# A nested Strassen step for the last setup product, and the rows of mp stored batch by batch in the loop: gated cross-attention with RMSNorm in fp32

## The chip, the cores and the metric

One core of a Trainium2 chip. The metric is the device time of one execution in microseconds (us), lower is better. All data and all arithmetic are fp32.

## The reference, cut to what matters

```python
# x: (8, 1024, 1024)   ctx: (8, 64, 512)   W_mem: (1024, 512)   W_gate: (1024, 2048)
mp     = einsum('bme,de->bmd', ctx, W_mem)                      # 8 x 64 rows of 1024
scores = einsum('bnd,bmd->bnm', x, mp) / sqrt(1024)
attn   = softmax(scores)
mctx   = einsum('bnm,bmd->bnd', attn, mp)
gate   = sigmoid(einsum('bnf,df->bnd', concat([x, mctx]), W_gate) + b_gate)
fused  = x + gate * mctx
out    = fused * rsqrt(mean(fused**2) + 1e-6) * norm_w          # norm_w is all ones
```

The half of the gate product that takes `mctx` is folded: `mg = mp @ W2` (W2 is the lower half of the transposed W_gate) is computed once for all 512 rows of memory, so that in the loop `attn @ mg` stands for `mctx @ W2`. What remains large is `x @ W1`, 8192 x 1024 x 1024.

## The kernel before, in words

**Setup** (to about 81 us). The memory is transposed on the TensorE. `mp` is then computed in transposed form, in four tiles `mpT[r][h]` (also called `m11`, `m12`, `m21`, `m22`), by one Strassen step of seven products (`pm_product`). `mg` is computed by a second one-level Strassen step, again seven products (`mg_product`, eight matmuls of 128x512 each), in the order 1, 6, 5, 2, 7, 4, 3, into the four tiles `c11`, `c12`, `c21`, `c22`. Its operands `t1`, `t2`, `b12` are sums of quarters of W2, which POOL makes (`w2_sum`), and `b21 - t2`, which DVE makes in place, in four pieces, ahead of product 4. The last product, number 3, is `s2` times `b22`, and is added to `c12`.

Beside that run the preparations of the loop. W1 is split into seven Strassen operands, of which four are outer sums: `outer_sum(5..)`, `(7..)`, `(6..)`, `(4..)`, one DVE instruction of 128x2048 each. Each operand `o` gets four inner sums for a second Strassen level, written to a tile `it{o}` (`inner_sum`, 128x512 each): for `o` = 1, 7, 5, 6, 4 on POOL in the setup, for 2 and 3 on DVE in the first pass of the loop. x comes in `xq` tiles of 512 rows (four transfers of 512 KB by `load_xq`); DVE transposes them in 32x32 blocks by STREAM_TRANSPOSE (`transpose_x`), eight instructions a tile, into `A` tiles that take the places of the `mpT` tiles in the setup. `outer_s` (DVE, 128x1024) and `inner_s` (POOL, 128x256) make the left sums.

**mp's two layouts in DRAM.** `store_mpT` writes the `mpT` tiles to the scratch `mpd`, from which `load_mp(b)` reads one batch for the scores. `store_mp(g)` transposes 128 rows (two batches) by two STREAM_TRANSPOSE on DVE and writes them by four DMAs of 128 KB into the scratch `mgd`; before, all four groups are done in the setup, between products 1 and 6. `store_mg` adds mg to `mgd`, and `load_mg(b)` brings both of a batch to the tile `mgs[b]`: rows of mp on partitions 0 to 63, rows of mg on 64 to 127.

**Loop.** Sixteen passes `q`, called quads, of 512 rows of x, two for each batch. A quad is seven outer products in the order 1, 6, 7, 5, 4, 2, 3; each is `outer_product`, an inner Strassen step of seven products A, B, C, D, A again, E, F, two matmuls of 128x256 each, and each such product is a *slot*; a quad has 49. Work of other engines is put by hand at slots (`at(t0 + 49, ...)` is the first slot of the next quad) or beside a product (`mid`). The five PSUM banks b0 to b4 take A to F in rotation, with F in the bank of B: so F can't start before DVE has made `u2` from B. In the first product of the first quad A, B, C, D, E take b0, b1, b2, b3, b4.

The setup's products take eight banks in turn (`setup_bank`): b0 to b4, two of the pool for contexts, and the one for scores. A product of the setup that uses b0 to b4 must therefore be read out before a quad's product of the same bank starts.

**Order.** All engines run what they are given in program order (`pin`). `mm` (line 92) is every matmul, `tt` (line 95) every tensor_tensor of DVE and POOL, `load` (line 98) every DMA of the SP queue, loads and stores alike. So the profile shows these three lines for nearly everything, and tiles must be told by their names: `pg` are the banks of mg's products, `mg_c` its four results, `t<-w,t` an outer sum, `it<-..` and some `t<-t`, `w<-w` an inner sum, `w<-w,t_w` the sums `b21 - t2`, `s<-..` an `outer_s`, `l<-..` an `inner_s`.

## Time and profile before

| | |
|---|---|
| median of 3 runs | 972.62 us (972.55 to 972.7) |
| the profiled execution | 972.56 us, its span 970.8 us |
| PE busy | 959.5 us, 99% of the span |
| DVE busy | 818.4 us, 84% |
| POOL busy | 761.1 us, 78% |
| ACT busy | 328.5 us, 34% |
| DMA moved | 128.32 MB |
| granted TensorE clock | 0.996 |

The span is what the profile sees of the profiled execution; 1.76 us of its time lie around it. PE is the TensorE's matmuls, PEld its weight loads, DVE the VectorE, ACT the ScalarE, POOL the GpSimd, SP the engine that issues the DMAs. A line of the timeline gives the start in us, the length in us, the engine, the line of the kernel, the operation, output<-inputs, shapes (partitions x elements) and count; where several instructions in a row are alike they are merged.

### The profile page before, as it was taken

The numbers are of one execution on the slowest core, as the hardware profiler recorded it, in microseconds if no ns is written. First come the engines' busy times: TensorE is split into PE (matmuls) and PEld (weight loads), VectorE is DVE, ScalarE is ACT, GpSimd is POOL, SyncE is SP. The second block draws the span as 40 slices with busy tenths as digits, with TensorE's granted clock in tenths as the row PEclk, the third lists the DMA queues.
The fourth block names the chain that finished last, engine by engine and source line by source line (L and its number), as shares of the span: only waits on it lengthen the run. The fifth ranks groups of instructions, "written<-read, shape, count | busy, mean of one in ns | idle before, by whom it ended". The sixth has DMA issues, their size and how long they took to land.

```text
span 970.8 us, 14402 instructions
## 1 busy us (share of the span) xinstructions
PE 959.5 (99%) x4986; PEld 774.9 (80%) x4986; DVE 818.4 (84%) x1482; ACT 328.5 (34%) x604; POOL 761.1 (78%) x889
## 2 busy tenths in 40 slices
PE   9999999999999999999999999999999999999995
PEld 8646878788888888788888888888887878888884
DVE  6988879879797988979797978979797978979787
ACT  2000234161423334161433324152333425152345
POOL 4997878778786978878786978878687878878692
PEclk9999999999999999999999999999999999999998
DMA  9856573482919374482918375381917465391712
GB/s 378 271 141 163 98 131 98 114 169 72 178 66 166 97 144 105 108 176 66 184 65 159 102 137 113 95 188 55 195 67 146 115 129 121 87 196 48 189 69 86
DMA packets 70919, 128.32 MB, mean 132 GB/s; under 512 B 12352, under 2 KB 49216, under 8 KB 70592
## 3 DMA queue, kind: packets, MB, share of 16 engines
q1 hardware_dynamic: 61520, 93.34, 37.0%
q0 software_dynamic: 9184, 33.56, 18.9%
q8 instruction: 39, 0.64, 0.3%
q10 hardware_dynamic: 144, 0.52, 0.1%
q14 instruction: 32, 0.26, 0.1%
HBM read 87.56 MB, written 41.68 MB: 133 GB/s over the span
## 4 chain that ended last, share of the span: by engine, by line
PE 98%; DVE 1%; issue 0%; ACT 0%; DVEq 0%
PE kA L92 20%; PE pc L92 12%; PE kE L92 11%; PE kD L92 10%; PE kF L92 10%; PE kB L92 10%; PE kC L92 10%; PE psT L92 6%; PE pg L92 5%; PE pm L92 3%; PE pz L92 0%; PE pa L443 0%; PE sc L417 0%; PE pt L196 0%; DVE gate L749 0%
## 5 line engine op out<-in xcount | busy, mean ns | idle before, releaser
L95 POOL TENSOR_TENSOR gate<-gate,u 128x256 f32<-128x256 f32 x336 | 287.5, 887 | 107.5 <-DVE u L95 107.5
L662 ACT ACTIVATE gate<-gate 128x512 f32<-128x512 f32 x128 | 80.5, 631 | 306.9 <-DVE gate L95 306.1
L349 DVE STREAM_TRANSPOSE a<-xq 128x512 f32<-128x512 f32 x128 | 137.9, 1099 | 2.7 <-POOL it L95 2.7
L95 POOL TENSOR_TENSOR l<-a 128x256 f32<-128x256 f32 x128 | 122.0, 953 | 21.6 <-PE kA L92 20.4
L92 PE MATMUL pc<-mg,attnT 64*128 64x256 f32 x512 | 127.5, 389 | 0.0
L92 PE MATMUL kB<-it,l 128*128 128x256 f32 x448 | 115.1, 379 | 0.2 <-DVE gate L95 0.2
L92 PE MATMUL kD<-it,l 128*128 128x256 f32 x448 | 115.0, 379 | 0.0
L92 PEld LDWEIGHTS pc<-mg,attnT 64*128 64x128 f32 x512 | 90.6, 186 | 29.9 <-issue 21.2
L691 DVE SCALAR_TENSOR_TENSOR gate<-gate,ss,nw_sb 128x512 f32<-128x512 f32 x120 | 110.6, 931 | 1.1
L95 POOL TENSOR_TENSOR l<-s 128x256 f32<-128x256 f32 x96 | 78.0, 813 | 36.1 <-PE kF L92 35.9
L92 PE MATMUL kA<-w,a 128*128 128x256 f32 x384 | 98.6, 379 | 0.0
L92 PEld LDWEIGHTS kB<-it,l 128*128 128x128 f32 x448 | 85.0, 190 | 12.1 <-DVE gate L95 0.6
L92 PEld LDWEIGHTS kD<-it,l 128*128 128x128 f32 x448 | 85.1, 190 | 11.6
L95 DVE TENSOR_TENSOR gate<-gate,pc 128x512 f32<-128x512 f32 x128 | 86.7, 678 | 0.4 <-ACT gate L662 0.4
L95 DVE TENSOR_TENSOR gate<-gate,kE 128x256 f32<-128x256 f32 x112 | 45.5, 419 | 47.1 <-PE kE L92 41.1
L92 PEld LDWEIGHTS kA<-w,a 128*128 128x128 f32 x384 | 71.7, 190 | 9.5 <-DVE s L95 0.2
L815 ACT COPY u<-kA 128x256 f32<-128x256 f32 x112 | 40.5, 361 | 110.3 <-PE kA L92 106.0
L92 PE MATMUL kE<-it,a 128*128 128x256 f32 x256 | 69.0, 392 | 0.0
L676 ACT ACTIVATE junk<-gate 128x1024 f32<-128x1024 f32 x60 | 63.5, 1058 | 10.5 <-DMA gate<-in_x 9.5
L92 PE MATMUL kA<-t,s 128*128 128x256 f32 x256 | 65.8, 379 | 0.0
L92 PE MATMUL kC<-w,l 128*128 128x256 f32 x256 | 65.7, 379 | 0.0
L92 PE MATMUL kF<-w,l 128*128 128x256 f32 x256 | 65.7, 379 | 0.0
(140 smaller groups left out, 2041.0 us busy)
## 6 DMA issues: line engine op xcount, KB each, us to landing
xq<-in_x SPq DMA_DIRECT2D x64, 512.0 KB, 10.3
gate<-in_x POOLq DMA_DIRECT2D x60, 512.0 KB, 8.1
out<-gate SPq DMA_DIRECT2D x60, 512.0 KB, 2.6
w<-in_w_gate_t SPq DMA_DIRECT2D x8, 512.0 KB, 10.0
w<-in_w_gate_t SPq DMA_DIRECT2D x2, 2048.0 KB, 17.1
mg<-mgd SPq DMA_DIRECT2D x16, 256.0 KB, 3.8
mpd<-mpT SPq DMA_DIRECT2D x4, 512.0 KB, 7.0
mgd<-mpq SPq DMA_DIRECT2D x16, 128.0 KB, 3.6
```

The lines of the kernel that those rows point to most:

```text
L92: pin(nc.tensor.matmul(o, lhsT, rhs, start=start, stop=stop, skip_group_check=True))
L95: pin(eng.tensor_tensor(o, a, b, op))
L349: nc.vector.transpose(A[key][:, :, r * P : (r + 1) * P], chunks(xq[q][:, 4 * t : 4 * t + 4, :], KD)[:, half * KH : (half + 1) * KH],)
L662: pin(nc.scalar.activation(g, g, AF.Sigmoid))
L676: nc.scalar.activation(junk, O[q, t], AF.Square, accum_out=ss[:, t % 2 : t % 2 + 1])
L691: nc.vector.scalar_tensor_tensor(g[:, cols], g[:, cols], rstd[:, t % 2 : t % 2 + 1], nw_sb[:, cols], ALU.mult, ALU.mult,)
L815: pin(nc.scalar.copy(p1, kb["A"]))
```

## The change

Four things.

1. The last product of mg, number 3, is computed by a nested Strassen step (`mg_nested`): its 256x512 by 512x512 blocks are cut once more into quarters, and seven products of two 128x256 matmuls take the place of eight 128x512 matmuls. Its right sums `t1_` to `t4_` are eight POOL instructions of 128x256, its left sums four on DVE, both in `it2` and `it3`. Its results are gathered by one ACT copy, three DVE sums from PSUM (`u2`, `u3`, `u4`), three POOL sums into `c12`, and four DVE sums from PSUM into `c12`. `outer_s(0, 1)` stands between the DVE's `u4` and these four.
2. Only the rows of batches 0 and 1 are transposed and stored in the setup (`store_mp_pair`: two STREAM_TRANSPOSE and four DMAs in place of eight and sixteen). The rows of batches 2 to 7 are transposed from the batch's tile `mps[b]` by one STREAM_TRANSPOSE at the slot at which `load_mg` stood, into a tile `mpq` of their own, and stored by four DMAs of 64 KB (`store_mp_batch`); `load_mg` comes a slot later, so that it and the next `load_xq` follow these stores in the SP queue.
3. `load_xq(0)` is issued ahead of the stores of `mpT`, and the first four `transpose_x(0, ..)` come before the sums of product 6.
4. The order of the inner sums: on POOL, `s3` comes before `it1`; `it7` comes after the first `inner_s`; the four of `it5` move from POOL to DVE, where they stand between the outer sum 6 and the sums of product 2.

```diff
-    inner_sums(nc.gpsimd, 1)                       # after the sums of W2 on POOL
...
+    load_xq(0)
     for r, h in ((0, 0), (1, 1), (1, 0)):
         store_mpT(r, h)
...
+    def store_mp_batch(b):
+        mpq = t4k(small, [P, M // 32, Q4], "mpq", f"mpq{b}")
+        pin(nc.vector.transpose(chunks(mpq, KD), mps[b]))
+        store_mp(mpq, slice(b * M, (b + 1) * M))
...
+    def mg_nested(eng, l, r, ts, ss, o):
...
+        for k in range(2):
+            tt(eng, t1_[:, k, :], r[k][:, hi], r[k][:, lo], ALU.subtract)
+            tt(eng, t2_[:, k, :], r[2 + k][:, hi], t1_[:, k, :], ALU.subtract)
+            tt(eng, t3_[:, k, :], r[2 + k][:, hi], r[k][:, hi], ALU.subtract)
+            tt(eng, t4_[:, k, :], r[2 + k][:, lo], t2_[:, k, :], ALU.subtract)
+        tt(nc.vector, s1_, l21, l22, ALU.add)
+        tt(nc.vector, s2_, s1_, l11, ALU.subtract)
+        tt(nc.vector, s3_, l11, l21, ALU.subtract)
+        tt(nc.vector, s4_, l12, s2_, ALU.subtract)
+        yield
...
+        kb = [setup_bank(f"pn{i}")[:, :C] for i in range(6)]
...
+        product(0, l11, r11)
+        pin(nc.scalar.copy(p1_, kb[0]))
+        product(1, s2_, t2_)
+        add(u2, p1_, kb[1])
+        product(2, s3_, t3_)
+        add(u3, u2, kb[2])
+        for n in (3, 2):
+            tt(nc.gpsimd, dst[n], dst[n], u3, ALU.add)
+        product(3, s1_, t1_)
+        add(u4, u2, kb[3])
+        tt(nc.gpsimd, dst[1], dst[1], u4, ALU.add)
+        product(0, l12, r21, False)
+        product(4, l22, t4_)
+        product(5, s4_, r22)
+        yield
+        for n, b in ((0, 0), (3, 3), (2, 4), (1, 5)):
+            add(dst[n], dst[n], kb[b])
...
-    for n in range(4):
-        inner_sum(nc.gpsimd, 7, n)
+    inner_sums(nc.gpsimd, 1)
...
-    for g in (2, 3, 0, 1):
-        store_mp(g)
+    store_mp_pair()
     load_mp(0)
+    for t in range(4):
+        transpose_x(0, t, 0)
     pgs = mg_product(6, s2, t2)
     mg_sum(c21, c11, pgs)
     tt(nc.gpsimd, s2, m12, s2, ALU.subtract)
-    for t in range(4):
-        transpose_x(0, t, 0)
     for part in range(2):
         inner_s(0, 1, part)
+    for n in range(4):
+        inner_sum(nc.gpsimd, 7, n)
...
+    next(nested)
     pgs = mg_product(5, s1, t1)
     mg_sum(c12, c21, pgs)
     w1_place(6)
     outer_sum(6, 3, 5)
     for n in range(4):
-        inner_sum(nc.gpsimd, 5, n)
+        inner_sum(nc.vector, 5, n)
...
+    next(nested)
     outer_s(0, 1)
-    pgs = mg_product(3, s2, b22)
-    mg_sum(c12, c12, pgs)
+    for _ in nested:
+        pass
     store_mg(c12, 0, 1)
...
-            at(t0 + 49, load_mg, (q + 1) // QPB)
+            if q + 1 > QPB:
+                at(t0 + 49, store_mp_batch, (q + 1) // QPB)
+            at(t0 + 50, load_mg, (q + 1) // QPB)
```

## The prediction

> **What bounds the kernel now.** I read the shares and the chain that ended last first, then PE's waits, and then the timelines of PE, DVE and POOL around 60 to 87 us, where the change lies.

> ```profile
> PE 959.5 (99%) x4986; PEld 774.9 (80%) x4986; DVE 818.4 (84%) x1482; ACT 328.5 (34%) x604; POOL 761.1 (78%) x889
> ...
> PE 98%; DVE 1%; issue 0%; ACT 0%; DVEq 0%
> ```

> The TensorE is the bound from end to end. PE's waits come to two entries, 1.2 us at the start and 0.2 us once: a PE instruction taken out is gained in full, and a PE wait added is lost in full.

> ```profile
> 67.61 7.03 PE L92 MATMUL pg<-w,mpT 128*128 128x512 f32 x16
> 74.48 7.03 PE L92 MATMUL pg<-w,mp_s 128*128 128x512 f32 x16
> 81.35 1.03 PE L92 MATMUL kA<-w,a 128*128 128x256 f32 x4
> 82.21 1.03 PE L92 MATMUL kB<-it,l 128*128 128x256 f32 x4
> 83.07 1.03 PE L92 MATMUL kC<-w,l 128*128 128x256 f32 x4
> ...
> 86.53 1.03 PE L92 MATMUL kF<-w,l 128*128 128x256 f32 x4
> ```

> The first line is product 4, the second is product 3, then the first quad begins. Starts tell the pace: product 3 takes 81.35 - 74.48 = 6.87 us, a product of the loop 0.863.

> ```profile
> 57.92 2.29 DVE L95 TENSOR_TENSOR t<-w,t 128x2048 f32<-128x2048 f32 x1
> 60.12 1.51 DVE L95 TENSOR_TENSOR mg_c<-mg_c,pg 128x512 f32<-128x512 f32 x2
> 61.55 6.19 DVE L95 TENSOR_TENSOR w<-w,t_w 128x512 f32<-128x512 f32 x4
> 67.78 3.24 DVE L95 TENSOR_TENSOR t<-w,t 128x2048 f32<-128x2048 f32 x1
> ...
> 83.33 0.42 DVE L95 TENSOR_TENSOR u<-u,kB 128x256 f32<-128x256 f32 x1
> 84.14 0.42 DVE L95 TENSOR_TENSOR u<-u,kC 128x256 f32<-128x256 f32 x1 [0.38 <-PE kC L92]
> 84.48 0.68 DVE L95 TENSOR_TENSOR it<-w 128x512 f32<-128x512 f32 x1
> ```

> ```profile
> 57.92 2.88 POOL L95 TENSOR_TENSOR l<-l,a 128x256 f32<-128x256 f32 x1
> 60.77 0.72 POOL L95 TENSOR_TENSOR l<-a 128x256 f32<-128x256 f32 x1
> ...
> 65.48 1.71 POOL L95 TENSOR_TENSOR t<-t 128x512 f32<-128x512 f32 x1
> ...
> 78.51 1.26 POOL L95 TENSOR_TENSOR t<-t 128x512 f32<-128x512 f32 x1
> 79.73 2.25 POOL L95 TENSOR_TENSOR it<-t,it 128x512 f32<-128x512 f32 x1
> 87.64 0.91 POOL L95 TENSOR_TENSOR l<-s 128x256 f32<-128x256 f32 x1 [5.65 <-PE kF L92]
> ```

> Two things. Neither engine has room here: DVE is busy without a break from 56.8 us to 83.8, POOL from 42.4 to 82.0. And they hinder each other: a DVE sum of 128x512 takes 0.68 us (84.48) where POOL idles, but the four at 61.55 take 6.19, 1.55 each; POOL's 1.26 at 78.51 is 1.71 at 65.48, and its `l`, 0.72, takes 2.88 beside a DVE sum of 128x2048. DVE's margin is thin: the four `w<-w,t_w` feed product 4 one each; the last ends at 67.74, product 4 starts at 67.61.

> [...] DVE alone 0.6 and POOL alone 1.2 (start to start) make 1.75 where they alternate. DVE sums with one input in PSUM keep their 0.6 to 0.7 beside POOL, transposes their 1.0. [...] the store of mpT issued at 17.95 landed at 34.9, behind norm_w (issued 14.6, landed 33.5).

> **The change part by part.**

> *PE.* Eight matmuls of 128x512 (6.87) go, seven products of 0.863 (6.04) come: **-0.83 us**. Nothing else changes on PE.

> [...] Before: twenty inner sums on POOL at 1.24 (24.8), `s3` and the update of `s2` at 2.33 (4.7), four `l` at 0.68 (2.7), and DVE's two outer sums (2.1 each), four `w<-w,t_w` (0.57 each) and `outer_s` (1.1): 39.8 us, so POOL should end `it4` at 82.2; the trace has 82.0. After: POOL sixteen inner sums 19.8, 4.7, 2.7, eight new sums of 128x256 at 0.68 (5.4); DVE four left sums (0.3 each), four inner sums of `it5` (0.57 each) and the same 7.6: 43.7 us, so POOL ends `it4` at about 85.4 to 86. [...]

> *DVE, step by step*, with alternation where both are at it. `xq` is issued at 23 (when DVE's last read of its place ends, 22.97), lands behind norm_w's 33.5 at 39 to 46, and is no longer waited for (before: to 52.7). Two transposes for mpq end at 43.2, four of x at 48.7 (they wait for POOL's `s3`, 44.8), sums of product 6 at 49.9; the left sums wait for POOL's `s2` (52.0) and end at 55.8; product 5's at 57.0; outer sum 6 at 60.4 (2.13 and a wait for POOL's current 1.2). Six removed transposes thus give nothing back here: DVE only waits elsewhere. Then `it5`: two at 1.76 beside POOL's `it7`, two at 1.2 beside POOL's new sums: 66.3. Product 2's sums, due at 60.8, end at 67.5. The four `w<-w,t_w` end at 68.2, 69.4, 70.6, 71.8. PE wants the first at 67.6 and the last at 70.2: **product 4 waits 1.66 us**, where the trace now has nothing.

> After that outer sum 4 (74.6), two transposes (76.5), six sums of products 7 and 4 (80.1), two transposes (82.0), `u2`, `u3`, `u4` (83.0), `outer_s(0,1)` (84.3), first sum into c12 (84.6). This frees b2, which kC of the first quad needs at 83.9: **0.76 us**. The next c12 sum waits for POOL, which comes to its three sums only after `it4` at 85.4: 86.1, 86.8, 87.5. DVE's last c12 sum ends at 88.0, `outer_s(0,2)` at 89.1, `u2` of the first quad at 89.4. kF needs it (bank b1) and stood at 88.1: **1.35 us**.

> These waits aren't independent: kF can't start before 89.4 whatever was lost earlier, against 86.53 before. So the sum is 1.66 + 0.76 + 1.35 - 0.83 = **+2.9 us**, and set by the end of `it4` on POOL; with 86.0 for it, +3.5. Behind kF come the scores' sixteen matmul pairs, 3.6 us in which DVE now waits 1.2; I find no further PE wait, and none of the loss is made up, as PE is the bound.

> *What only moves.* `load_xq(0)` passes three stores of mpT in SP's queue; the four stores now land behind it, at 45 to 48. They are waited for by the x transposes, which take mpT's places (44.8 and, for the second pair, 46.7: up to 2 us late, while DVE waits for `s2` until 52.0 anyway), and by load_mp(0), whose scores come at 90. On POOL `it1` now ends at 49.7 (wanted at 83), `it7` at 63.3 (wanted by the third outer product, near 101), `it6` at 79.4 (95), `it4` at 85.4 (115): all hidden. ACT's one new copy (0.37) falls where ACT idles.

> *c12's way to mg.* The store goes out at 88.4, lands 2.8 later, load_mg 3.8 after that: 95.2; POOL issues the bias at about 98 (before 94.1), landing 7.2 later at 105; PE wants it at 110.8. Hidden, 5 us to spare. xq of quad 1 goes out at 92 to 94, lands 12 later, wanted at 112.

> *The loop.* Six transposes of 1.0 us at a quad's first slot (quads 4, 6, ... 14). In quad 4, DVE has gaps of 0.3 and 1.0 us at 308.3 and 309.4, before PE needs its F at 310; it is hidden. SP's queue: stores issued at about 306.8 to 308.5, landed at 312, load_mg, then xq at 313 to 315 in place of 300.9 to 303. xq lands 10 us after issue (median), so at 325; DVE wants it at 328.5. Hidden with 3 us to spare; mg, wanted after 327, lands at 317. If that cover failed, DVE would wait the excess six times. Bounds: 0 to 1 us each; a gain is excluded, as PE doesn't wait there now. I take 0.

> Against the profiled execution, 972.56 us (0.06 below the median of the runs, so the two can be used alike): 972.56 + 3.0, taken between the two figures for `it4`, is **975.6 us**.

> **The rivals.** (a) *Everything new is hidden*, -0.83: 971.7. For it: PE waits for nothing today, an `it5` sum costs DVE only 0.68 alone, and DVE no longer stands still for xq. [...] It decides where the last `w<-w,t_w` ends before 70.2 and `u2` before 85.7, 3.7 us earlier than I find. A part of it (POOL ends `it4` by 84) gives a change under 1.9, no measurable one. (b) *The loop pays*: xq of the even quads comes late. In the trace its last transfer took 18.1 us from issue when it shared the DMAs with the residual's; with this at 314.5 it lands at 332, 4 us late, some 3 after DVE's slack. At 1 us for each of six quads 975.6 becomes 981.6. Against it: the residual's 1 MB now goes first. (c) [...] +1 to +2, about 974. (d) The nested product could lose more, if xq landed after 49: then DVE's transposes start late, 977.3.

> **How the numbers follow.** The forecast (975.6, own range 974.6 to 976.8) gets 0.66, (c) 0.13, (a) 0.08, (b) 0.06, (d) 0.07. A measurement can tell 0.2%, 1.95 us, from no change. Faster by that much is in no case that I can work out (the most is 0.83): 0.02 out of (a). Same takes the other 0.06 of (a), 0.12 of (c) and 0.02 of the forecast's lower end; slower has the rest, 0.78. Range 973.2 to 978.2, without (b) and most of (a).

> **What would show it.** Right: PE's waits name `pg` <- DVE `w` (1 to 2 us), `kC` <- DVE and `kF` <- DVE; the nested products start near 76 and take 6.0; POOL's `it<-t,it` ends at 85 to 86 and its `mg_c` sums follow at once; `it<-t` sums of DVE take over 1 us each. Wrong: kF at 86 or earlier, or DVE waiting for `xq` around slot 26 of quads 4, 6, 8.

## The result: 1032.15 us, 6.2% slower, and the profile after

| | before | after |
|---|---|---|
| median of 6 runs | 972.37 us (971.96 to 972.7) | 1032.15 us (1031.07 to 1033.53) |
| the profiled execution, its span | 972.56, 970.8 us | 1032.27, 1030.5 us |
| granted TensorE clock | 0.996 | 0.977 |

The ratio is 1.0617, with a 95% interval from 1.0605 to 1.0628. The forecast was 975.6 us, range 973.2 to 978.2: the side was right, the size was not. In the page after, the shares and the chain that ended last read:

```profile
PE 974.6 (95%) x4998; PEld 786.2 (76%) x4998; DVE 826.3 (80%) x1495; ACT 328.5 (32%) x605; POOL 764.1 (74%) x896
...
PE 82%; DMA 8%; POOL 5%; DVE 3%; issue 1%; ACT 0%; DVEq 0%; POOLq 0%
...
L95 DVE TENSOR_TENSOR gate<-gate,kA 128x256 f32<-128x256 f32 x112 | 44.0, 405 | 54.0 <-DMA out<-gate 52.5
```

PE is no longer the whole chain: 8% is a transfer, and the third line, a group of DVE's, says which: DVE stood still 52.5 us for `out<-gate`, the store of finished rows. PE's waits, all of them (in total, times, longest):

```profile
PE kB L92 <- DVE gate L95: 42.2, 7, 7.7
PE kC L92 <- DVE mg_c L95: 1.3, 1, 1.3
PE pz L92 <- DVE zeros L118: 1.2, 1, 1.2
PE kF L92 <- DVE u L95: 1.1, 1, 1.1
```

The second and the fourth are the two waits forecast at the seam of setup and loop. The first is new, and is nearly everything. I measured each quad from its first `psT` (the scores' matmuls, once in a quad) to the next one's. Before, quads 1 to 14 take 54.85 us, one of them 55.04; after, quads 4, 6, 8, 10, 12 and 14 take 63.72, 64.71, 64.85, 64.23, 64.54 and 64.70, the others 54.85. That is +57.65 us in the loop, and the first `psT` starts 1.97 us later (89.45 against 87.48): 59.6 together, and the spans differ by 59.7.

**Quad 4.** SP's queue first, before and after (start, length in which it issues, what). Before:

```profile
299.69 1.10 SPq L98 DMA_DIRECT2D mg<-mgd  x2
300.88 2.13 SPq L98 DMA_DIRECT2D xq<-in_x  x4
316.77 5.66 SPq L98 DMA_DIRECT2D out<-gate  x2
```

After:

```profile
308.74 1.75 SPq L98 DMA_DIRECT2D mgd<-mpq  x4
314.23 1.13 SPq L98 DMA_DIRECT2D mg<-mgd  x2
315.41 2.23 SPq L98 DMA_DIRECT2D xq<-in_x  x4
318.76 5.66 SPq L98 DMA_DIRECT2D out<-gate  x2
```

SP is held twice. The four stores stand ahead of `load_mg` in its program and need the transpose of that slot, which DVE ends at 308.7; and `load_mg` reads what they write, so SP waits for their landing, from 310.5 to 314.2. Everything in its queue waits with it: `xq` goes out 14.5 us later than before. Of these, 2.0 are the later start of the loop, some 7 the wait for the transpose's slot, and 5.5 the issue and the landing of the stores. The next in SP's program is the store of a finished row of quad 3. Before, it followed `xq` by 14 us, and landed in 4.9 us, at 321.69; DVE needed that row's buffer, one of seven for `gate`, at 322.04. So the slack was 0.35 us. Now it is issued 1.1 us after the last of the four `xq` transfers of 512 KB, none of which has landed (they land at 322.95 to 330.89). The piece of it in the chain of waits, and then DVE's timeline around the wait:

```profile
318.76 13.17 DMA out<-gate
```

```profile
323.28 0.75 DVE L756 SCALAR_TENSOR_TENSOR gate<-gate,ss,nw_sb 128x512 f32<-128x512 f32 x1
332.02 0.42 DVE L95 TENSOR_TENSOR gate<-gate,kA 128x256 f32<-128x256 f32 x1 [7.99 <-DMA out<-gate]
332.36 0.41 DVE L95 TENSOR_TENSOR gate<-gate,kD 128x256 f32<-128x256 f32 x1
```

The store takes 13.17 us. DVE, in order, can't write into the new `gate` until it lands; the sums behind that one read PE's banks, so PE soon finds its bank for kB still full:

```profile
325.56 1.03 PE L92 MATMUL kA<-t,s 128*128 128x256 f32 x4
332.83 2.07 PE L92 MATMUL kB<-it,l 128*128 128x256 f32 x4 [6.25 <-DVE gate L95]
334.70 1.91 PE L92 MATMUL kC<-t,l 128*128 128x256 f32 x4
336.40 1.64 PE L92 MATMUL kD<-it,l 128*128 128x256 f32 x4
337.88 1.03 PE L92 MATMUL kA<-t,s 128*128 128x256 f32 x4
```

PE idles 6.25 us, and there is a second loss behind it: kB, kC and kD take about twice what they took before. The windows show why (PE's busy time stands first, and the column after POOL's is the granted clock):

```profile
327.40:330.81 3.41, 0.00 (x0) 0.00 (x0) 0.00 (x0) 0.95 (x1) 0.00 (x0) 1.00 1.11 241
330.81:334.22 3.41, 1.39 (x3) 1.17 (x4) 2.20 (x4) 0.00 (x0) 2.05 (x3) 0.50 0.47 192
334.22:337.64 3.42, 3.42 (x9) 2.66 (x8) 2.78 (x7) 0.00 (x0) 1.41 (x2) 0.50 0.00 0
337.64:341.05 3.41, 3.41 (x23) 2.51 (x22) 2.97 (x5) 0.00 (x0) 3.41 (x6) 1.00 0.02 5
```

The granted clock halves at 330.81, while PE still waits, and comes back at 337.64: PE runs at half its clock for 4.8 us after the wait, and for 4.2 to 5.1 us after all six. The windows above count in steps of 3.41 us: an idle step, a half-clock step in which PE is idle for 2.02 us, a half-clock step that PE fills, and then the full clock. That the steps are fixed is seen from all six: the half-clock stretches are 6.83 us long, two steps, and start 119.46 to 119.47 us apart, which is 35 steps, while the waits end at uneven distances (119.64, 119.94, 118.70, 119.30 and 119.63). The six idles are 6.25, 7.32, 7.70, 6.69, 6.92 and 7.17 us, 42.0 together. Of the other 15.6 of the 57.65, 2.6 for each, the half clock makes about 14.3 (half of the time after each wait). PE's busy time on the page, 974.6 against 959.5, is up by about that.

### The profile page after: what moved, and what is told of

Read it like the earlier page. It is cut to its first block, busy times and chain, and to the rows that moved or that the text cites. A ratio compares the mean times of both kernels' runs of the same rounds, so it can differ in the third digit from the quotient of the medians.

```text
span 1030.5 us, 14470 instructions
## 1 busy us (share of the span) xinstructions
PE 974.6 (95%) x4998; PEld 786.2 (76%) x4998; DVE 826.3 (80%) x1495; ACT 328.5 (32%) x605; POOL 764.1 (74%) x896
## 4 chain that ended last, share of the span: by engine, by line
PE 82%; DMA 8%; POOL 5%; DVE 3%; issue 1%; ACT 0%; DVEq 0%; POOLq 0%
PE kA L92 17%; PE pc L92 11%; PE kB L92 10%; PE kE L92 9%; PE kC L92 9%; PE kD L92 9%; PE kF L92 8%; DMA out<-gate 8%; PE psT L92 6%; PE pm L92 2%; POOL it L95 2%; POOL w L95 1%; POOL mg_it L95 1%; DVE gate L756 1%; DVE gate L95 1%
## 5 line engine op out<-in xcount | busy, mean ns | idle before, releaser
L95 POOL TENSOR_TENSOR gate<-gate,u 128x256 f32<-128x256 f32 x336 | 287.2, 885 | 164.3 <-DVE u L95 123.1
L92 PE MATMUL kB<-it,l 128*128 128x256 f32 x448 | 121.4, 395 | 42.2 <-DVE gate L95 42.2
L95 POOL TENSOR_TENSOR l<-a 128x256 f32<-128x256 f32 x128 | 113.4, 886 | 23.9 <-PE kA L92 21.0
L92 PEld LDWEIGHTS kB<-it,l 128*128 128x128 f32 x448 | 87.5, 197 | 57.0 <-DVE gate L95 45.1
L92 PE MATMUL pc<-mg,attnT 64*128 64x256 f32 x512 | 127.5, 389 | 0.0
L92 PE MATMUL kD<-it,l 128*128 128x256 f32 x448 | 118.5, 388 | 0.0
L92 PEld LDWEIGHTS pc<-mg,attnT 64*128 64x128 f32 x512 | 90.6, 186 | 29.9 <-issue 21.2
L95 POOL TENSOR_TENSOR l<-s 128x256 f32<-128x256 f32 x96 | 78.2, 815 | 34.2 <-PE kF L92 32.4
L92 PE MATMUL kA<-w,a 128*128 128x256 f32 x384 | 98.6, 379 | 0.0
L92 PEld LDWEIGHTS kD<-it,l 128*128 128x128 f32 x448 | 88.4, 197 | 13.1
L95 DVE TENSOR_TENSOR gate<-gate,kA 128x256 f32<-128x256 f32 x112 | 44.0, 405 | 54.0 <-DMA out<-gate 52.5
L95 DVE TENSOR_TENSOR gate<-gate,pc 128x512 f32<-128x512 f32 x128 | 86.5, 676 | 0.4 <-ACT gate L727 0.4
L95 DVE TENSOR_TENSOR gate<-gate,kE 128x256 f32<-128x256 f32 x112 | 45.4, 417 | 48.6 <-PE kE L92 43.1
L92 PEld LDWEIGHTS kA<-w,a 128*128 128x128 f32 x384 | 71.7, 190 | 9.1
L92 PE MATMUL kE<-it,a 128*128 128x256 f32 x256 | 69.0, 392 | 0.0
L92 PE MATMUL kC<-w,l 128*128 128x256 f32 x256 | 65.8, 379 | 1.3 <-DVE mg_c L95 1.3
L92 PE MATMUL kF<-w,l 128*128 128x256 f32 x256 | 65.8, 379 | 1.1 <-DVE u L95 1.1
L92 PE MATMUL kA<-t,s 128*128 128x256 f32 x256 | 65.8, 379 | 0.0
```

The lines of the kernel that those rows point to most:

```text
L92: pin(nc.tensor.matmul(o, lhsT, rhs, start=start, stop=stop, skip_group_check=True))
L95: pin(eng.tensor_tensor(o, a, b, op))
```

## The experiments

All times are medians, each compared with the kernel before on the same chip; those medians are 972.13 to 972.25 us.

**1. The kernel before, with the stores in the loop alone.**

```diff
+    def store_mp_batch(b):
...
-    for g in (2, 3, 0, 1):
-        store_mp(g)
+    store_mp(0)
...
-            at(t0 + 49, load_mg, (q + 1) // QPB)
+            if q + 1 > QPB:
+                at(t0 + 49, store_mp_batch, (q + 1) // QPB)
+            at(t0 + 50, load_mg, (q + 1) // QPB)
```

> The kernel before with the stores of mp's rows of batches 2 to 7 moved into the loop as in the change (same slots), and nothing else of the change: no nested product, old order of the sums on POOL and DVE, xq 0 loaded where it was. My theory: the whole loss of the changed kernel in the loop (six quads longer by 8.9 to 10.0 us, 57.6 us together) comes from this part, because SP waits for the stores of mp's rows, so xq goes out 14 us later and the store of out that frees a gate buffer queues behind its 2 MB. Then this kernel takes 972.4 + 57 = 1029 us (1024 to 1034), with six PE waits of 6 to 8 us at kB of the fourth outer product. Rival (the setup's new order or the nested product carries the loss into the loop): 972 to 976.

1029.46 us, ratio 1.0589 (1.0568 to 1.0610). The six quads take 63.14, 64.08, 64.63, 64.11, 64.81 and 64.92 us. PE's waits, all of them:

```profile
PE kB L92 <- DVE gate L95: 42.0, 6, 7.7
PE pz L92 <- DVE zeros L118: 1.2, 1, 1.2
```

The loss in the loop comes with this part alone, and the waits of kC and kF to the rest of the change.

**2. The change, with the stores of `out` issued by ACT**, so that they don't stand behind `xq` in SP's queue.

```diff
-            load(out[b, n0 : n0 + P, :], g)
+            pin(nc.scalar.dma_start(out[b, n0 : n0 + P, :], g))
```

> The changed kernel with the stores of out issued by ACT in place of SP (the last quad's excepted), all else as changed: xq is as late as before. If the store of out lands late [...], it now shares the DMA engines with xq instead and lands some 5 us after issue: the six waits shrink from 7 us to 0 to 2, 975 to 990 us, less what ACT loses by standing at these issues. Rival (the DMA engines are simply busy, in whatever queue): the waits stay at 5 to 8 us, 1020 or more. Rival 2 (DVE waits for xq itself, not for a gate buffer): no change, 1030.

1001.18 us, ratio 1.0298 (1.0277 to 1.0319): half of the loss is gone, and more was expected. The store of quad 4, issued at 320.56, landed after 9.2 us in place of 13.2, and 4.3 us ahead of the last of `xq` instead of behind it; the idles of kB are 2.29 to 2.95 us. From 322 to 333 us the packets' times on the sixteen DMA engines, as the profile adds them up, come to 81.1% for SP's queue and 27.3% for ACT's: freed from the order of SP's queue, the store still moved beside `xq`, and took 9.2 us where it had taken 4.9 before the change. So I read the order as a part of the cause, and the 2 MB in flight as the other. There is a cost of its own as well: the quads without such an idle take 55.32 (the first of them 55.86), where one kA starts 0.33 us later than in experiment 4's second run and one kC 0.14. The list of waits names ACT's copy `u` ahead of kA, once, 0.6 us; what delays the copy was not shown. I had not counted that cost.

This run has idles just at the edge of the slow clock. Those of 2.29, 2.39, 2.43 and 2.84 us cost only themselves, against 55.32; those of 2.55 and 2.95 us cost 1.5 us more each. The length doesn't decide, but the fixed steps do. The half-clock stretches here are one step of 3.41 us (their starts, 558.08 and 899.41, lie 100 steps apart). The steps around the idles of 2.39 and of 2.55 us:

```profile
442.03:445.44 3.41, 1.71 (x8) 1.53 (x9) 2.52 (x5) 3.17 (x7) 2.37 (x3) 1.00 1.09 309
445.44:448.86 3.42, 3.42 (x24) 2.77 (x24) 3.32 (x9) 0.00 (x0) 1.41 (x3) 1.00 0.29 73
554.67:558.08 3.41, 1.12 (x5) 1.02 (x6) 1.93 (x4) 3.30 (x8) 1.79 (x3) 1.00 1.08 315
558.08:561.49 3.41, 3.41 (x10) 2.71 (x9) 3.11 (x8) 0.23 (x1) 1.40 (x2) 0.50 0.25 78
```

A step with 1.70 us of idle is followed by the full clock, one with 2.29 by the half. The idle of 2.84 us fell into two steps, 1.64 and 1.20 us, and cost nothing more; that of 2.95 left 2.62 in one. Laid over the traces of before and after, from 10 us on, such steps agree: each full-clock step with 2.14 us of idle or more (2.14 is the step of before in which PE ends, at 959.61) was followed by a half one, and none with 1.85 or less. So an idle of PE need not fill the step: the 2.29 us of 3.41 at 554.67 were followed by the half clock.

**3. The change, with eight buffers for `gate` in place of seven.** For the room, `norm_w` (all ones) is kept as a single element that is used for all columns.

```diff
-    gpool = ctx.enter_context(tc.tile_pool(name="gpool", bufs=7))
+    gpool = ctx.enter_context(tc.tile_pool(name="gpool", bufs=8))
...
-    nw_sb = const.tile([P, D], F32, name="nw_sb")
-    load(nw_sb, norm_w.partition_broadcast(P))
+    nw_sb = const.tile([P, 1], F32, name="nw_sb")
+    load(nw_sb, norm_w[0:1].partition_broadcast(P))
+    nw_b = nw_sb.to_broadcast([P, 512])
...
-                nw_sb[:, cols],
+                nw_b,
```

> The changed kernel with eight gate buffers in place of seven. Room for it comes from norm_w, of which one element is read and used for all columns (inputs: all ones). xq and the store of out are as late as in the changed kernel. If the wait is for the buffer that this store frees, DVE doesn't meet it: no PE wait at kB of the fourth outer product, 974 to 978 us. Rival (DVE or POOL wait for something else that is late, xq or mg): 1015 to 1032.

978.63 us, ratio 1.0066 (1.0046 to 1.0086). SP's queue is as late as in the change (`xq` at 316.23, the store at 319.31), yet PE doesn't idle at that kB at all. So it is the buffer that PE waited for, by way of DVE, and a late store is harmless with one more of them. What is left in the even quads, 55.00 to 55.77 us, is the wait that rival (b) named: in quad 6 DVE waits 0.88 us for `xq` up to 441.97, and a later kB of PE, at 445.43, 0.25 us for DVE's next sums. In the list of DVE's waits of this run:

```profile
DVE a L349 <- DMA xq<-in_x: 4.2, 5, 1.3
```

In the change itself the longer wait before it covers this one.

**4. The change, with the transpose and its stores at an earlier slot of the quad before**: 24, and then 33.

```diff
-                at(t0 + 49, store_mp_batch, (q + 1) // QPB)
+                at(t0 + 24, store_mp_batch, (q + 1) // QPB)
```

> The changed kernel with the transpose and the store of a batch's rows at slot 24 of the quad before (they need only mp of that batch, loaded at slot 10), load_mg where it is. By my theory the stores have long landed when load_mg comes, SP doesn't wait, xq goes out at its old time, and the six long quads fall back to 54.85 us: 974.3 us (973.5 to 975.5), the setup's +2.0 being left. Rival 1 (the extra DVE transpose, or the 24 extra DMAs themselves, cost it): stays above 1000. Rival 2 (the store of out is only moved behind another transfer): 980 to 1000.

977.48 us, ratio 1.0055 (1.0038 to 1.0071).

> The changed kernel with the transpose and store of a batch's rows at slot 33 of the quad before. At slot 24 the transpose cost PE 0.42 us in each of six quads; DVE has gaps of 0.4 us at 284.1 and 284.9, about slot 33. My theory: the transpose is hidden there or costs under 0.2 us, the quads are 54.85 to 55.05 us, in all 974.3 us (973.8 to 975.3), the setup's +2.0 being all that is left. Rival (a transpose on DVE costs PE its 0.4 us wherever it is put): 976.8 to 977.5.

974.86 us, ratio 1.0030 (1.0019 to 1.0042). SP's queue in quad 4 of the second:

```profile
286.93 1.76 SPq L98 DMA_DIRECT2D mgd<-mpq  x4
301.48 1.10 SPq L98 DMA_DIRECT2D mg<-mgd  x2
302.67 2.15 SPq L98 DMA_DIRECT2D xq<-in_x  x4
318.55 5.66 SPq L98 DMA_DIRECT2D out<-gate  x2
```

The stores have landed long before `load_mg`, `xq` goes out as before, and all long quads are gone, with ACT, the buffers and the order of `xq` and `out` in the queue untouched. With slot 24 the six odd quads, in which the transpose now stands, take 55.26 to 55.29: it costs PE some 0.42 us in each, 2.5 us in all. At slot 33 it costs nothing that can be seen; one quad takes 54.95, all others from quad 1 on 54.85. So the forecast's "hidden" was right of the transpose itself, where it stands well, and wrong of the queue. What is left in the second run, a first `psT` at 89.25, is the setup's part.

**5. That, with product 3 plain again.**

```diff
-    for _ in nested:
-        pass
+    pgs = mg_product(3, s2, b22)
+    mg_sum(c12, c12, pgs)
```

(and without `mg_nested` and the two `next(nested)`).

> As s33, with product 3 as eight matmuls of 128x512 again (no nested step, none of its sums), the new order of the rest kept. My theory (the nested step saves PE 0.83 us, and its eight sums on POOL, four on DVE and the four that gather it make kC and kF wait 2.3 us): kC and kF wait for nothing or under 0.5 us, 1.0 to 1.5 us less than s33, about 973. Rival (the waits come from the four sums of it5 on DVE and the new order, whatever the product is): kC and kF still wait, and PE needs 0.83 more: 0.8 us more than s33, about 975.

972.33 us, ratio 1.0001 (0.9993 to 1.0009). There are no waits of kC or kF, and the first `psT` starts at 86.82. So the nested step's sums make these waits: it gives PE 0.83 us and costs a net 2.5 here. What is left of the change (the new order, and the stores in the loop at slot 33) makes no difference that can be measured.

**6. Can the nested step be had without its waits?** Four variants of the second run of 4.

(a) The four sums of `it5` back on POOL:

```diff
-        inner_sum(nc.vector, 5, n)
+        inner_sum(nc.gpsimd, 5, n)
```

> As s33, with the four inner sums of it5 on POOL again. My theory ([...] the end of it4 on POOL sets kF): POOL has 5.0 us more[...], so it4 ends 2.6 us later, kF waits so much longer: 976.9 (976 to 978). Rival (DVE's own length sets the waits; POOL is not on the path): DVE is 5 to 7 us shorter ahead of product 4, kC's wait goes, about 972.5 to 973.5.

979.95 us, ratio 1.0082 (1.0068 to 1.0095). The wait of kC goes, but POOL's `it4` ends at 87.55, its sums into c12 come after, and DVE stands in order behind them:

```profile
88.26 0.42 DVE L95 TENSOR_TENSOR mg_c<-mg_c,pn 128x256 f32<-128x256 f32 x1 [7.75 <-POOL mg_c L95]
```

```profile
91.58 2.07 PE L92 MATMUL kF<-w,l 128*128 128x256 f32 x4 [6.29 <-DVE u L95]
93.58 4.94 PE L92 MATMUL psT<-a,mpb 128*64 128x256 f32 x32
```

kF waits 6.29 us, and the slow clock shows again, granted at 0.50 from 91.5 to 95: 2.07 for kF, and 4.94 for the 32 `psT` that take 3.67 elsewhere. In direction as expected (`it4` ends 3.4 us later than in the second run of 4, where 2.6 was expected, from 5.0 us more on POOL and 2.3 less on DVE), larger in size; the slow clock is a part of that.

(b) POOL's three sums into c12 ahead of `it4`, and DVE's first ahead of `outer_s(0, 1)`:

```diff
-    for o in (6, 4):
-        for n in range(4):
-            inner_sum(nc.gpsimd, o, n)
+    for n in range(4):
+        inner_sum(nc.gpsimd, 6, n)
```

(with the sums of `it4` after the nested step's products and POOL's three sums, ahead of `outer_s(0, 1)`, and `add(dst[0], dst[0], kb[0])` ahead of them.)

> As s33, with POOL's three sums into c12 ahead of it4's four inner sums, and DVE's first sum into c12 ahead of outer_s(0, 1). My theory: kC's bank comes free before PE is there and u2 no longer stands behind it4, so both waits go or shrink to under 0.5 us in all, and the nested step's 0.83 us are left as a gain: 971.4 to 972.2, against 972.1 before. Rival ([...] DVE's sums now wait for it4 in the quad): the waits come back at kF or at the second outer product, 973.5 to 974.5.

976.43 us, ratio 1.0044 (1.0032 to 1.0057), 1.6 us more than without this order, and 2 us above the rival's range. The wait of kC in the seam is gone, but others have come; PE's waits in the seam and the first quad:

```profile
PE kF L92 <- DVE u L95: 1.2, 1, 1.2
PE kC L92 <- POOL l L95: 0.8, 2, 0.4
PE kB L92 <- POOL l L95: 0.6, 1, 0.6
PE kB L92 <- DVE gate L95: 0.6, 1, 0.6
```

(c) As (b), with `it4` at slot 18 of the first quad, since it is read only from slot 28; (d) as (c), with DVE's sums of `it3` at slots 30 to 33 in place of 22 to 25, so that the two series don't stand beside each other.

```diff
+    for n in range(4):
+        at(18, inner_sum, nc.gpsimd, 4, n)
...
-        at((3, 4, 5, 6, 22, 23, 24, 25)[i], inner_sum, nc.vector, o, n)
+        at((3, 4, 5, 6, 30, 31, 32, 33)[i], inner_sum, nc.vector, o, n)
```

> The order of `reorder` (POOL's three sums into c12 and DVE's first one come earlier), and the four inner sums of it4 on POOL go from the setup to slot 18 of the first quad, as it4 is read only by the fifth outer product, from slot 28. Theory ([...] with 6 us of it moved behind kF both waits go, and the nested product's 0.83 us is gained at last): the first psT near 86.7, the loop as in s33, about 971.5 to 972.0, at most 0.1% faster than the kernel before. Rival ([...] POOL idles some 6 us before its first l, and hardly later, so it4 comes late for the fifth outer product or slows DVE's sums of it2 and it3): a wait of PE at kB of the fifth outer product (o=4) of 1 to 4 us, 973 to 976.

976.77 us, ratio 1.0047 (1.0035 to 1.0059).

> As it4_late, and the four sums of it3 on DVE go from slots 22 to 25 of the first quad to slots 30 to 33, so that they don't stand beside it4 on POOL. Theory: if it4_late loses time to the two series of sums holding each other up, this gives it back: 971.5 to 972.2. Rival [...]: as it4_late within 0.5 us, the waits of PE only moved to the later outer products of the first quad.

975.59 us, ratio 1.0042 (1.0030 to 1.0054). PE's waits for (d):

```profile
PE kC L92 <- POOL l L95: 1.8, 1, 1.8
PE pz L92 <- DVE zeros L118: 1.2, 1, 1.2
PE kB L92 <- DVE gate L95: 0.9, 1, 0.9
PE kF L92 <- DVE u L95: 0.5, 1, 0.5
```

The first `psT` does start earlier in (c) and (d), at 87.45 and 87.04 in place of 89.25, but the next interval is 51.61 and 50.36 in place of 47.54. The rivals' waits came both times: they went from the seam into the first quad, to POOL's `l` and DVE's sums (from 90 to 140 us of (d) POOL was busy 43.6 us of 50 and DVE 42.2). In (c) they are at kB of the fifth outer product (1.2 us), where the rival had put them, and at a kC and a kD as well, so that the time is 0.8 us above its range. In (d) the median is 1.2 us lower; the runs of the two overlap (976.66 to 977.52, 975.04 to 978.75), so that this is not shown. No version here beats the kernel before. A place outside the first quad for POOL's sums was not tried.

## Why the prediction was wrong, point by point

- **The step that failed: "The loop. ... I take 0".** It costs 57.65 us. The dates of issue in that step were good: stores at 306.8 to 308.5, `xq` at 313 to 315 (measured 308.7 to 310.5, and 315.4, in a trace that runs 2 us later). But the step asked only who waits for `xq` and `mg`, and not what stands behind `xq` in SP's queue. That is the store of `out`. The pieces were at hand: `xq` landing near 325 and, in the setup, a store of mpT that landed at 34.9 behind norm_w's 33.5 in SP's queue, both in the forecast; the store at 316.77 in the trace of before. Put together, if it lands behind `xq` as that one did behind norm_w, the store lands after 325 at the earliest, where DVE needs its buffer at 322.04: a wait of several us in each of six quads. The order was read in the setup and applied there alone. The cover for `xq` itself was mis-sized too: "xq lands 10 us after issue (median)" is the time of a middle one of its four transfers, and each transpose of DVE's reads all four. The last landed 13.8 us after issue, at 330.89, where DVE's wish, 328.5 and 2 us of shift, was 330.5: nothing to spare in place of 3 us.
- **The second part of the miss**, about a quarter of the loop's, is the clock. PE's longest wait in the trace of before is 1.2 us, and the forecast priced every wait at its own length; six waits of 7 us cost 9.6 each.
- **Rival (b)** named the right place, the right quads and the right cause, SP held up by the stores. Its victim was wrong (`xq` itself, where it is the store behind it), and its price too: 1 us for each quad, against 9.6. Its own wait exists: experiment 3 shows it at 4.2 us of DVE's time in five places, and 2.9 us over the six quads.
- **PE's gain**: -0.83 forecast; the nested products run from 74.40 to 80.44, 6.04 us, where the plain one took 6.87. Right.
- **Product 4**: a wait of 1.66 us forecast, about 0.2 measured (7.22 us long in place of 7.03). The mis-sized term is when DVE comes to outer sum 6: it started at 56.30 and ended at 58.5, where the steps gave 57.0 and 60.4; the wait for POOL of 1.2 us that was put there did not come. The sums of `it5` took 6.15 us (58.50 to 64.65), where 5.9 was worked out, and the last `w<-w,t_w` ended at 69.95 rather than 71.8.
- **kC and kF**: 0.76 and 1.35 us forecast, 1.28 and 1.05 measured, by the path that was given: POOL ended `it4` at 84.35 (85.4 to 86 forecast), its c12 sums followed at once, and `u2` ended at 88.3 (89.4). Net, the first quad starts 1.97 us later, where +2.9 was forecast. Experiments 4 and 5 show this part by itself: 974.86 us with a loop that costs nothing, 972.33 without the nested step. Had the loop been free, the time would have lain in the forecast's range, on its low side: what is left of the loss there, 1.9 us in the profiled executions and 2.7 in the medians, lies between the forecast's +2.9 and rival (c)'s +1 to +2, for which DVE and POOL would hold each other up less than by taking full turns.
- **The ledger of DVE's and POOL's times**, added up as if each waited for the other (an estimate from the trace of before), served well: it put the end of `it4` within 1.7 us, and experiment 6 goes its way: work moved by some slots came back as waits elsewhere, and `it5` moved from DVE to POOL, where an inner sum alone takes 1.23 us, start to start, in place of 0.60, put the end of `it4` off by 3.4 us. The forecast's 1.75 us for a sum of each in turn was 1.67 both before (POOL from 65.48 to 68.83) and after (59.67 to 63.01).

## What to carry to other kernels

When a step puts a store and a load that reads it into an engine's DMA queue, ask when the store's data is there and when the store lands, list everything behind the two in that queue, loads and stores alike, and look for the buffer that each store gives back: a buffer with 0.35 us of slack turned one held-up queue into a wait of 7 us of PE's per quad, and an earlier issue (slot 33 of the quad before) removed it whole. A TensorE wait of 6 us or more in the loop cost its length and some 2.6 us more here; through the waits of 1.28 and 1.05 us at the seam the granted clock stayed at 1.00. Before moving work off a tight stretch, check that the engine it goes to has room there, and that what runs beside it does too: here a DVE sum of 128x512 took 0.68 us where POOL idled and 1.55 beside POOL's sums.
